# Square roots without ScalarE's table and a causal mask on the exponentials, in a four-layer kernel with a baked order

## The chip, the cores and the metric

The kernel runs on one core of one Trainium2 chip, in one launch. The metric is the device time in microseconds (us). The engines are TensorE (PE, with its weight loads PEld), VectorE (DVE), ScalarE (ACT), GpSimd (POOL) and SyncE (SP, which issues most transfers).

## The reference, cut to what matters

The input is two sequences of 1024 tokens with 128 features, in fp32. Four layers follow each other; each takes the layer norm of x and adds a product of two branches:

```python
for layer in range(4):
    xn = layernorm(x)                  # 1 / sqrt(var + 1e-5)
    s  = attention_branch[layer](xn)
    g  = silu(feedforward_branch[layer](xn))
    x  = x + s * g
```

- Layer 0: a delta-rule attention in chunks of 32 tokens with q and k of unit length, `beta = sigmoid(xn @ Wb)`, short convolutions, a router that mixes four outputs, and RMS norms; its other branch has silu and gelu.
- Layer 1: softmax attention with 16 heads of 8 features, with scores divided by a Frobenius norm (a root), and a mixture of eight experts, two per token.
- Layer 2: linear attention with 16 heads of 64, and a small transformer on 63 chosen tokens with RMS norms.
- Layer 3: causal attention with 16 heads of 64 that share k and v, q and k of unit length, and two blocks of windowed attention with rotary positions, norms of q and k, a layer norm and a gated gelu.

The causal attention of layer 3 is where the mask of this change lies:

```python
q, k = l2norm(q) * 4, l2norm(k) * 4
sim  = einsum('bhid,bjd->bhij', q, k)
sim  = where(j > i, -max, sim)
out  = einsum('bhij,bjd->bhid', softmax(sim), v)
```

## The kernel before, in words

**Recording and order.** The program does not issue instructions as it is written. Each call is recorded as a unit (`Record.note`, line 507; up to 32 matmuls of one kind make one unit), with the tiles that it reads and writes. The units are then issued in an order that is baked into the source as a compressed string (`ORDER`), which a search outside the kernel has found; it also says, for each evacuation that either engine can do (`Ctx.evac`, line 710), whether DVE or ACT does it. A second string (`PLACES`) says which buffer each tile takes. `Record.issue` (line 571) reads both, so nearly every instruction of the profile has line 591. Batch 0 and batch 1, and the two branches of a layer, are interleaved by this order; on each engine the instructions run in it. Each engine class in `Engines` (line 616) has a fixed and a per-element cost for that search, and `TABLES` names the activation functions that need a table of ACT: exp, gelu, silu and sin, sqrt, sigmoid.

**Roots.** `Ctx.rstd` (line 759) and `Ctx.rnorm` (line 766) form one over a root: DVE adds or clamps, ACT takes `Sqrt`, DVE takes the reciprocal. They are used by `layernorm` (line 773; eight columns, 12 times), in layer 0 (the norm of q and k with 64 columns, line 843, and `rms` with 32), in layer 2's `rmsnorm` (one column), in layer 3's causal attention (`rnorm` of k with 4 columns, of q with 64 columns in `Block.scale`), and in layer 3's feed-forward branch (q and k norms with 64 columns in `ss`, and `root` with 4 columns before `roots`). Layer 1 has two single roots on one row (`den`, `q2`). ACT holds one table at a time, so a root between exponentials or gelus needs an `ACT_TABLE_LOAD` before and after it.

**The causal attention.** `l3_attn` (line 1832) goes block of queries by block (`Block(i)`, 512 queries, i = 0, 1) and in each through eight pairs of heads (`pair(p)`). For each tile m of 128 keys up to the diagonal, `scores(m)` makes two score tiles `sim` in PSUM (one for each head of the pair, on half of the array's rows), adds the mask `hide` (0 or -1e30) on DVE to the first 128 columns if the tile is on the diagonal, and lets ACT write the exponential to `e` in SBUF. `sums(m)` multiplies `e` into `num` (a half of the array's columns for each head) and adds `e` to the running total on DVE. Scores of tile m + 1 come ahead of the sums of tile m:

```python
if m >= 4 * i:
    nc.vector.tensor_tensor(ps[a][:, :P], ps[a][:, :P], C.c["hide"], ALU.add)
nc.scalar.activation(es[a][:, :n], ps[a][:, :n], AF.Exp, scale=16.0)
```

There are 2 batches x 2 blocks x 8 pairs x 4 diagonal tiles x 2 heads = 256 such additions. Beside them layer 3's feed-forward branch has its rotation on POOL (`sq`, `u`, 128 and 64 products).

**Layer 0's recurrence.** Each chunk's state follows from the last: four small matmuls `next` on PE, then an addition `state` on DVE, 30 times in each batch. `chunk`, `pu` and `out` are the small matmuls around it.

Of the kernel before, what the change touches and what calls it, by code (L numbers as in the profile page):

```python
# [25 lines left out]
P = 128  # L26
NB = 2
# [172 lines left out]
def _constants():  # L200
# [20 lines left out]
        "hide": np.where(p <= c, 0, -1e30) + 0 * one,  # L221
# [13 lines left out]
        "token": p + P * c[:, :8],  # L235
        "slot": np.where(c < 127, c, -1) + 0 * p,
# [32 lines left out]
def pack_inputs(inputs):  # L269
# [31 lines left out]
TABLES = {AF.Exp: 1, AF.Gelu: 2, AF.Gelu_apprx_tanh: 2, AF.Silu: 3, AF.Sin: 3, AF.Sqrt: 4, AF.Sigmoid: 5}  # L301
# [6 lines left out]
    "c-n1R2V4`$+uqsT6hiNysDQ}XMNm<&on7pLT~G9n1$#wLgaqt@4J)2{cF%%X5DRv|Q&Fs_AfgnJqI3c&yYtP=CJ^rTkz{vgcFNo4dEObdFY(O(YmCLR-|6"  # L308
    "r6zU_|EzXRPL!>Sq4<a1pL{bL+Xk2B|LIdk)T=F$ZFlBZ+nqWJ0cj|yks?PYSWFd((ai60%Kai>R0RngN->g=oOzZ~;Jpk;xxvgkq1-0KS%ZS!xnR`u@Sv"
    "(fR%HKxkWxu?UwmL)`RZ$R5D*hR^(mLoQM(W5qUp7;B_cZNB?Wij-xU5-0mbcNZ#uJo^MjPz~$kD=QR%sVI!0wK)yQY%(kJOAi`xzfeaK(c(LqsZ<haEP4"  # L310
    "~veoH(OI3;Uq&AzM`NUR^cgL!Xz77ojp2)ce`sc~#d#Cze?zVkkcHY`n3&3C=CRp~l7t-yhU($`iFz5_q>Yw)-dMjn%%Hoo>s+d1}zpNN?#%0!$y*axV#<"
    "a?F)6nDZ)ecV{RcRyvDvha1vvA}fvF7*JwWf8_*u$?5iI>Js1GVNx8kMn%XEkmz@QHJI<(b#YsQ$ZCAxAsu<oN0e@_3h0JMA~%48V_O#r4iKB=wnX0my8N"
    "uQ{z-K63rku0;W8@@HO^>kPiRJnLz!1hQ1mNB!>&`s{8}D;5tvXP(~@<lUY-93~y|_8hSZh8CUxb1nJkC6oT4V^*=-=2_KSZ(6e*7=s0hHOFWF4d%yg{d1"
    "neDCtY^(vcG`-929scpj)XfUq#hr*;`P*3@SW{F&Vgl-8MK3Ufy&BHU)4T)Tbh8S#oqm$_LRmvk1tGO;fKZtJ(N+zLQhozr))d!>{1*PabU$dC4$>n?CW1"
    "d42VO)azJueoJWV~@}7_dO@M-~A6RTc%L5+0K!6^w0z#9^x6LHq8ur)F0d{l&Lw<_T5G5(q_#H>SCCe_t>d1`CVc{a>UEu+y*6HQ!W>ptcVRx9dH1od+E&"
    "5{v!Z^Ck*T~_A0*K8)V;WF#yA)18&_M-Dk!eW2YTMhu)N38z@#;C40sBncrBlua~)W#Patmc6+{c8_sXLGQd{T`dzPnww0P*Per@9)f&H>M}iL(SuPaqQE"
    "jX?J2hLXmAV<j*@36FjJhnwlYDlczcc;9-q**bShB48hs0=~v2sb-g}JQrSJ$^)3b*fhqw>x_7%3W+07iO6KJk6g9i;RD$$i1UKB)I6z_h88eHxo-R{hbm"
    "#WxpJmC-Rvtfbq$?b0f-;|FmYfMOt{V@AhM?b3PxWNl#kQ?I2}IWQJi01y!O#zXQP^ca5YxmBCtciwmM3ztV4FP7|`r#uZno9r`>4?7eCD_MyaShF=eUu?"
    "s&KNm%Gs02Z^7XbSsBu)hwAm#u&`dw#ml>rVf^Lns=jqnF+w*j)MOwyJnfluvTbf*F6{|ErJgcfN<T8T&tYMK?MEsa^dV@Yc7n3ZW}EwVtTbmnt`Cu7kr%"
    "~b96Cf<An0O1>m#Pegfe-?pyCg|`nI+Ff#`~Co1Nu3x->KK;yeY%w1qg}P<LkF*P^TVsgy~v#I@@>zuJ)qt(EJXaoHwawGTz5I>7#Mp?SsHYI($6Hnn^Vp"  # L320
    "YzB-=oKgR^@ns0okmu<;2(6h!~Yx%|Xbr*}rof1wTZ+0rM*y5j4*Vumm7-1wnKPI)`#Q>haI{wO}O5_TW)-D0`NCRNx4PaJd)!~`hFNqegD&Y0T`?Z$gMI"
    "Ntcn)ZB!?Bo8??F++zSt;2f;9yy0#Z{Th>Yj_RT4{@)2NaYPIx>NWC3MGkmUW+-S=D#=1l>z3L8XORhY$6#2mO^Iz_rZvyG6Hj{|wAOJ{u2AYE>4o16rsG"
    "I@L=Us5DXW%ug!`y?ah<NQ%$<x~TIXz`n!&7oyP&i}!~_5eqKfFH$c*@4p|g^I~nl=wk~G0iKy3yFg28jJaWV811kdQkvDE5|An(XT^zrnb(=qT(yx{$wA"
    "9XV5v0bL|V=mGFr$>adc@~LzPjUBPZgdxppH`IG$(39L>=6x$Wqj`rov+Z=AI@bfp<x&Oi|l(Hp??#*D1W0wA8K)rdLSl~Ds$_@zXEq(uKDpPQ3-(YcZ4b"
    "gj&|Oy=^D;U^{lY5Nz@sMeCpbufY&EtBtLRS9_7a)I2A(f%|xbNZoSZL`f-8&JYPmba+pt>$klm6~VR0=tY(D}g9V!>kRlHmVS@GKd7Vsxn801rNO7nf6{"
    "UJwz`+#tarRkTX%4BDGimSjcJ^<TXaayy~H0qE<35dh**gtEAQSV&fevv<y_e?-D;Y$F2L)Ud}}i2l5UTD%w^1oIVg)+>L#-HX%c@JScbR=>8gzJl)HVe-"
    "u!5#H#Y%px=gO7w!tCC+0bAo;h_>zui9;?N9CfWRv*cD@%7X@k=+D&)7fLKF`#C(BbwzF3C4<``Pq(<CyCk<^OK><e^Mpz|I3-=xIf*in96M&CQLKcQaQd"
    "h-fWi9kywGVN$14+RROpPPM+V*=)k&6H`4PShJm)b{1)~`6&C@=X2j8#}`VIx{s%K03|g2Wwqkyw~ZSenJ-3Bt5inUGvSV6X_&{X6L9>Azzt#X0cH!_Jv^"
    "oybK)1vS?gtrvs38sO>orH5)(Km!EWklm2BR@O6i;<#&t7JYApj#O+PRvj#o~PQwLmNWPpK2KV?_Z5@VF{{*|`>__zG#T3BK1%$x6fee`9ISw}P5W^<yBA"
    "60ceuYH@v*H10Ge|>&iL@*B>zc0STjK8t}=Ebx7-pFbztfU!M)4n_1Dw{U+4mfFFTbnlA?>c*X*vAzK35VmQe*CdnN1gehx9G{`cPIY5X*BBEphrC1u~f>"  # L330
    "?lomuUlfL$3_&4pP8^SqJ_&Q^)UBp6B=mwEW^tkuZgR<J?F+W;Y{yHt^Rofz}X$F{=Gr){dN=?f(_H?D%NNHchJ{%#dF*R2HjaI%DQq4Xa@n@wI&GC|4r<"
    ")^ann5v716e(!jrn?`kFE^-;+osJT+E_nq5){JRGNac_N%vLF1ouW%Dh_)=qh{C%eX$Zy9K;3rTWIyUltcEd#8@zZug>}47=^~udmrH;A5ExdRVx8Oz!_E"
    "DA)cB7}V`)3m`5wOZO^~f_l@Mv~DuC%(^DWjny2QYqyEzoW@x|$ViKtp`fM29ILJ~fv(>;$qq34tCNi5%`+Wo^N-CXM!=|EV*zQSB9nSsy2QRrOTX*P%hI"
    "}`u-5|1Y6h(lr4i&IFLNy69d8fIb|`!}M#ChCHB*%7T}2$r7umBSj;2or?p|7SCor?^iY>)^Hb%)4eRlTpOH1tFoH!DGEAC}mkl5|z+;3%eSADFCdS3NNZ"
    "`L#4zO{U2dGtzCW6Mvb_ndOY6T7or_bxcx!pGn8!l9U@TYI=%Sl6dMA#)9A1}u*~2wk*)(J(9DG0!Z23z{|{oQ`N6M(^z(|J%$?=g!5Rv3wl+zY~}JKffC"
    "dxIFM%*40J8!sM6D6W^GEkc(X|PJGt$Li<iH7w(+)ZOPnD?SgyfEc^cS>#wcF4}VXdcx5Wj_+K`zlO34?LU%vwbnJhB^?5wTrS9O1bLsb|Hs907;mVBclz"
    "?LQ8hcRKy!vzNs-LZuo5NJ+PbNwV?EFpy-W~kd)brI3Q9(+d=+keagO+t#-D*T_r;RN=UwH=3YEfkDac#^I7mIq;z_^Yzv@-Tos?DZ<-gmjD$jbw-^A{fL"
    "FG}v^Q2by@QvL{s%Tvp$-+Djq-0G~%^X}NI*0n0X=Y7=oz>u2zlkR<U>HMkAv+`}<w^b5V-(=Ou8*_>tmn|-M+EMiOm#l8al}Yh+eUqmi=|1q+#!>I5*Ea"
    "`y=&JdzvwzsN1z*NnmjSEYGvDxE++DLZy|*uuNx<zM|BmSM=coAfA3BWdb~SCoprvEN{I;#AdOpx-%bI)Yf%ki)?L6_}#rF`qWZ$ApQR|%6Ic*T8Z<=wpl"
    "gIK?@7rlhEKO6Nd!+{-g7p0Av(JMM1+U!r0Zhm_=zZhHGv6mKfmgc!<+^`nAK%#Zb@qfyZpK}FpJlXX)(jq;wJanXbpF({vR7=TUl&W!-Nco7t!{UIHS@8"  # L340
    "t(l^8FD6RT8Dsk5Lq6$m=>5z99w*BU}e&0urH-Y_>KKGgBTQZk=Zjt`c9(=G~v8(dL(rr72p4nQvc*UuoV0j8yGQ;Oz(CcY08<)LH_Wm8``rI~QiR*H}nC"
    "^(3pAB};cKvEr?Xk-!OS8QCfsu84qg}y97bbzUH<mOUrj{g6%ddFf(=}gJm*I7CbxP-g=t%QtH4H!S{+JIfe<_Vy<)?a><orEsMCC)#t-T-Xyf3wU;$d|B"
    "kS6`wq;d=6y5^Oc?my3m|J|;xHTdDNZMZ}8{UfScmi+5%^i}2i(pBly<pA(D`uaFLu{>z|NcNlTGpIIeVfhZ>bGs`;bANi;yaTHqTizL4nBV2v+HFgsCBI"
# [12 lines left out]
    "Q{4*c+A>;jO=+#awl*9JAn<p@B+T7?hA~)G)=vzzr@^8&~rq3Ij<kYzz#NNG5cD-imoyzx4^G;@cjgnt2e!_M-x?IJ}_&r|zMKEb}VsDKE$l^zoTiqGMGj"
    "+5`{jS22Rz#GSSr53{y!Ul5bleqMd&7Uk|BeNNp?N(!t=j^Er7>{Llvf`-KlB(G!TUN~2|9Kv&t<cTpJ;WTF<)MF@mMtH-LePor&jTn=Enleb8O-V-l=De"
    "KDIC(lsMe-%;=j##Tv$}a*ta8E$(+OJ$HPwq8IM=7P(fB3dcB9h%Qw?38OVZ+fjDm_p26_gSyLC@w@Ev*YUf>H2wg(|D!o}ML8G#Y@XQl?cfmq9`fb3b+2"
    "3Jb^^wKMwWf;`gj0>gQNjk5l9`F>3+wh+!}t>j{NMVdhPoJ)YK15DVgy|tWoxT_c^foa!22vrb&)&vPV74m5lUpPez(rW$FH<YjR(e$~>*JjJ`Tn!=y5$W"
# [266 lines left out]
class Ctx:  # L626
# [132 lines left out]
    def rstd(self, out, ss, scale, eps):  # L759

        nc = self.nc
        nc.vector.tensor_scalar(out, ss, float(scale), float(eps), ALU.mult, ALU.add)
        nc.scalar.activation(out, out, AF.Sqrt)
        nc.vector.reciprocal(out, out)
# [1555 lines left out]
```

## Time and profile before

| | |
|---|---|
| median of 3 runs | 1816.81 us (1807.41 to 1821.72) |
| profiled execution | 1815.64 us, span 1813.9 us |
| mean granted TensorE clock | 0.967 |
| busy PE / PEld | 1700.4 / 956.8 us |
| busy DVE / ACT / POOL | 1270.4 / 1045.7 / 417.9 us |
| `ACT_TABLE_LOAD` | 101, 1283 ns each |
| mask additions `sim<-sim,const` on DVE | 256, 293 ns each |
| sums `e<-e` on DVE (128 to 512 columns) | 320, 167.0 us in all |

In a line of the profile the line number and the engine come first, then the operation, the tile that is written and those that are read, the shapes, the count, and after the bars the busy time with the mean of one in ns, and the engine's idle time before these instructions with what ended it. In the rows of 40 slices a digit is the busy share in tenths. An fp32 matmul shows as two passes and a transpose as one, so 7750 instructions are 14500 records. Passes of matmuls overlap in the records.

### The profile page before, as it was taken

The page shows a single profiled execution, that of the slowest core. Times are in us where ns is not written, and L with a number is a line of the kernel's source. Part 1 is how long each engine was busy: PE and PEld are TensorE (multiplying, and loading weights), DVE is VectorE, ACT ScalarE, POOL GpSimd, SP SyncE. Part 2 cuts the span into 40 slices and gives each one's busy share as a digit, 9 for nine tenths or more (in the row PEclk, how much of TensorE's full clock was granted, in tenths as well). Part 3 has the DMA queues.
Part 4 walks back from the last instruction along what each step waited for, and adds up shares of the span by engine and source line. Part 5 has one row for each costly group of instructions (what it writes and reads, how often), then busy time and mean ns, then how long its engine had stood idle before and what let it go on. Part 6 is the DMA issues. An engine that isn't in the chain of part 4 may idle for free. (4 is left out here: it accounts for less than half of the span.)

```text
span 1813.9 us, 36041 instructions
## 1 busy us (share of the span) xinstructions
PE 1700.4 (94%) x14500; PEld 956.8 (53%) x14500; DVE 1270.4 (70%) x2546; ACT 1045.7 (58%) x1907; POOL 417.9 (23%) x450
## 2 busy tenths in 40 slices
PE   7997998798999999999988989999999899999998
PEld 4464445565234943358455457753436567643376
DVE  7855587476212634425889989978798989887875
ACT  4221452246888579865646546576555668775653
POOL 1110013002502245112211253040601740540000
PEclk9996999788999999999999989999999999999999
DMA  2110002000503224224131123202004231001131
GB/s 109 21 31 3 0 7 42 15 1 20 170 12 115 71 81 104 69 84 146 28 109 33 46 60 100 69 12 61 4 1 112 69 83 52 4 4 46 24 95 37
DMA packets 82407, 97.55 MB, mean 54 GB/s; under 512 B 39584, under 2 KB 51872, under 8 KB 82112
## 3 DMA queue, kind: packets, MB, share of 16 engines
q1 hardware_dynamic: 73120, 65.92, 13.1%
q0 software_dynamic: 9120, 29.33, 5.8%
q8 instruction: 114, 1.87, 0.4%
q14 instruction: 53, 0.43, 0.1%
HBM read 79.84 MB, written 6.98 MB: 48 GB/s over the span
## 5 line engine op out<-in xcount | busy, mean ns | idle before, releaser
L591 ACT ACTIVATE e<-sim 128x512 f32<-128x512 f32 (+3 forms) x896 | 428.5, 561 | 151.9 <-PE sim L591 59.6
L591 DVE TENSOR_TENSOR e<-e 128x512 f32<-128x512 f32 (+3 forms) x320 | 167.0, 547 | 13.9 <-ACT e L591 6.2
L591 PE MATMUL num<-e,v 128*64 128x64 f32 (+4 forms) x1280 | 168.7, 386 | 0.4 <-ACT e L591 0.2
L591 ACT ACT_TABLE_LOAD x101 | 129.6, 1283 | 53.3 <-PE sim L591 8.8
L591 PE MATMUL sim<-q,k 32*128 32x512 f32 x1024 | 156.2, 636 | 2.9 <-DVE place L591 1.2
L591 PE MATMUL sim<-q,kT 64*128 64x512 f32 (+3 forms) x768 | 149.4, 511 | 3.1 <-ACT e L591 1.8
L591 POOL TENSOR_TENSOR sq<-qk,tab 128x256 f32<-128x256 f32 x128 | 102.5, 824 | 166.3 <-DVE ss L591 135.1
L591 PE MATMUL av<-e,va 128*32 128x512 f32 x1024 | 130.7, 602 | 0.0
L591 PEld LDWEIGHTS num<-e,v 128*64 128x64 f32 x1280 | 75.6, 137 | 85.7 <-issue 66.5
L591 PE MATMUL ph<-h,w_f 128*128 128x512 f32 x256 | 117.7, 616 | 3.1 <-ACT h L591 2.3
L591 PEld LDWEIGHTS sim<-q,kT 64*128 64x128 f32 x768 | 66.8, 186 | 82.9 <-ACT e L591 49.3
L591 PEld LDWEIGHTS sim<-q,k 32*128 32x128 f32 x1024 | 48.8, 183 | 93.8 <-ACT e L591 73.3
L591 POOL TENSOR_TENSOR u<-u,sq 128x512 f32<-128x512 f32 x64 | 85.4, 1349 | 1.6
L591 DVE TENSOR_TENSOR sim<-sim,const 128x128 f32<-128x128 f32 x256 | 65.7, 293 | 27.4 <-PE sim L591 25.4
L591 DVE SCALAR_TENSOR_TENSOR conv<-vT,w_a,conv 128x1024 f32<-128x1024 f32 x60 | 82.9, 1389 | 1.3
L591 PEld LDWEIGHTS ph<-h,w_f 128*128 128x128 f32 x256 | 49.3, 197 | 63.2 <-issue 57.8
L591 POOL DMA_INDIRECT xg<-xd,token x46 | 45.3, 985 | 139.8 <-ACT e L591 102.8
L591 ACT ACTIVATE e<-e 128x512 f32<-128x512 f32 x96 | 57.0, 625 | 26.2 <-DVE e L591 25.6
L591 DVE COPY asb<-av 128x512 f32<-128x512 f32 x16 | 11.0, 685 | 84.1 <-PE av L591 75.5
L591 PEld LDWEIGHTS av<-e,va 128*32 128x32 f32 x1024 | 23.6, 108 | 81.2 <-issue 68.1
L591 ACT ACTIVATE h<-ph,w_f 128x512 f32<-128x512 f32 x32 | 21.2, 687 | 78.2 <-PE ph L591 78.2
L591 PE MATMUL qk<-w_f,shifted 128*128 128x512 f32 x128 | 62.9, 608 | 2.7 <-DVE shifted L591 1.4
(543 smaller groups left out, 3523.2 us busy)
## 6 DMA issues: line engine op xcount, KB each, us to landing
zb<-zd SPq DMA_DIRECT2D x192, 128.0 KB
w<-v SPq DMA_DIRECT2D x60, 128.0 KB
tab<-in_rotary SPq DMA_DIRECT2D x8, 512.0 KB
yd<-y SPq DMA_DIRECT2D x10, 256.0 KB
w_f<-in_f SPq DMA_DIRECT2D x4, 512.0 KB
w_l<-in_l SPq DMA_DIRECT2D x4, 512.0 KB
mk<-in_mask SPq DMA_DIRECT2D x4, 512.0 KB
w_f<-in_f SPq DMA_DIRECT2D x4, 448.0 KB
```

The source lines that it names most:

```text
L591: tc.keep_in_program_order(f(*map(real, args), **{k: real(v) for k, v in kw.items()}))
```

## The change

1. `rstd` becomes two instructions on POOL: add epsilon, then raise to the power -1/2 against a new constant `mhalf`. The scale 1/n goes into the `Square` activation ahead of it. `rnorm` does the same for up to eight columns (k's norm); for 64 columns it clamps on DVE and calls `rsqrt`.
2. `rsqrt` is new: a first value from the bits of the number (a multiply-add on them as an integer), then three Newton steps of three DVE instructions each. It serves q's norms in layer 3, and the norm and `rms` of layer 0.
3. Layer 1's two roots become powers with `phalf` on POOL; one of them, and the mean square of layer 3's `root`, is copied from PSUM by DVE first.
4. Layer 0's sigmoid is written as (1 + tanh(x/2))/2. `Sqrt` and `Sigmoid` leave `TABLES`.
5. The mask of the causal attention moves behind the exponential: POOL's `affine_select` writes 0 where the key is later than the query. The constant `hide` goes.
6. `ORDER` and `PLACES` are new strings for the new set of units; all units stand in a new order, and 16 more evacuations are on ACT in place of DVE. `Record.issue` passes on a bit cast.

```diff
-TABLES = {AF.Exp: 1, AF.Gelu: 2, AF.Gelu_apprx_tanh: 2, AF.Silu: 3, AF.Sin: 3, AF.Sqrt: 4, AF.Sigmoid: 5}
+TABLES = {AF.Exp: 1, AF.Gelu: 2, AF.Gelu_apprx_tanh: 2, AF.Silu: 3, AF.Sin: 3}
...
-    def rstd(self, out, ss, scale, eps):
+    def rstd(self, out, ss, eps):
+
+        nc, n = self.nc, ss.shape[-1]
+        nc.gpsimd.tensor_scalar(out, ss, float(eps), None, ALU.add)
+        nc.gpsimd.tensor_tensor(out, out, self.c["mhalf"][:, :n], ALU.pow)
+
+    def rnorm(self, out, ss, floor):
+
+        nc, n = self.nc, ss.shape[-1]
+        if n <= 8:
+            nc.gpsimd.tensor_scalar(out, ss, float(floor), None, ALU.max)
+            nc.gpsimd.tensor_tensor(out, out, self.c["mhalf"][:, :n], ALU.pow)
+            return
+        x = self.small("x", n)
+        nc.vector.tensor_scalar_max(x, ss, float(floor))
+        self.rsqrt(out, x)
+
+    def rsqrt(self, out, x):
 
         nc = self.nc
-        nc.vector.tensor_scalar(out, ss, float(scale), float(eps), ALU.mult, ALU.add)
-        nc.scalar.activation(out, out, AF.Sqrt)
-        nc.vector.reciprocal(out, out)
-
-    def rnorm(self, out, ss, floor):
-
-        nc = self.nc
-        nc.vector.tensor_scalar_max(out, ss, float(floor))
-        nc.scalar.activation(out, out, AF.Sqrt)
-        nc.vector.reciprocal(out, out)
+        t = self.small("t", x.shape[-1])
+        nc.vector.tensor_scalar(out.bitcast(I32), x.bitcast(I32), -0.5, 1597463007.0, ALU.mult, ALU.add)
+        for _ in range(3):
+            nc.vector.scalar_tensor_tensor(t, out, -0.5, out, ALU.mult, ALU.mult)
+            nc.vector.tensor_mul(t, t, x)
+            nc.vector.scalar_tensor_tensor(out, t, 1.5, out, ALU.add, ALU.mult)
...
-    nc.scalar.activation(beta, psb[:, :NTH], AF.Sigmoid)
-    nc.vector.tensor_mul(beta, beta, rk)
-    nc.vector.tensor_mul(beta, beta, rk)
+    nc.scalar.activation(beta, psb[:, :NTH], AF.Tanh, scale=0.5)
+    nc.vector.scalar_tensor_tensor(beta, beta, 1.0, rk, ALU.add, ALU.mult)
+    nc.vector.scalar_tensor_tensor(beta, beta, 0.5, rk, ALU.mult, ALU.mult)
...
-    nc.scalar.activation(q2, q2, AF.Sqrt)
+    nc.gpsimd.tensor_tensor(q2, q2, C.c["phalf"][:1], ALU.pow)
...
                 for a in range(2):
+                    nc.scalar.activation(es[a][:, :n], ps[a][:, :n], AF.Exp, scale=16.0)
                     if m >= 4 * i:
-                        nc.vector.tensor_tensor(ps[a][:, :P], ps[a][:, :P], C.c["hide"], ALU.add)
-                    nc.scalar.activation(es[a][:, :n], ps[a][:, :n], AF.Exp, scale=16.0)
+                        nc.gpsimd.affine_select(
+                            out=es[a][:, :P], in_=es[a][:, :P], compare_op=ALU.is_ge, fill=0.0, base=0,
+                            pattern=[[1, P]], channel_multiplier=-1,
+                        )
...
-            C.rstd(r, pn[:, :4], 1.0, 1e-5)
+            nc.vector.tensor_copy(r, pn[:, :4])
+            C.rstd(r, r, 1e-5)
```

## The prediction

> **What bounds the kernel now.** I read the page's first two parts, then the windows by layer, then the PE timeline inside two stages, and last the chain and the groups. From the page:
>
> ```profile
> PE 1700.4 (94%) x14500; PEld 956.8 (53%) x14500; DVE 1270.4 (70%) x2546; ACT 1045.7 (58%) x1907; POOL 417.9 (23%) x450
> ...
> PE   7997998798999999999988989999999899999998
> ...
> DVE  7855587476212634425889989978798989887875
> ACT  4221452246888579865646546576555668775653
> POOL 1110013002502245112211253040601740540000
> PEclk9996999788999999999999989999999999999999
> ```
>
> PE is nearly always busy, but busy is not streaming. In the PE timeline 15 passes of ph (128x512) end 6.60 us after the first starts, and one lasts 0.62, so a full pass costs (6.60 - 0.62)/14 = 0.43 us; 16 passes of 128x128 take 1.95 us, so 0.11 each. Counting all 14,500 passes of the groups by form at this rate, a tile of a quarter of the array at a quarter, gives 1447 us. So 1814 - 1447 = 367 us are lost, only 114 of them shown as idle. The windows say where (layer 0, 1, 2, 3, then the two spans that hold the 256 masks of layer 3's causal attention):
>
> ```profile
> 0.00:450.00 450.00, 394.49 (x4632) 235.50 (x4632) 304.93 (x603) 155.36 (x244) 54.72 (x71) 0.90 0.11 25
> 450.00:850.00 400.00, 396.48 (x3084) 194.70 (x3084) 152.60 (x369) 303.37 (x565) 114.66 (x123) 1.00 0.32 92
> 850.00:1150.00 300.00, 273.07 (x1745) 167.23 (x1743) 264.87 (x475) 173.44 (x288) 80.93 (x79) 0.97 0.24 67
> 1150.00:1814.00 664.00, 636.33 (x5043) 359.36 (x5043) 547.97 (x1100) 413.54 (x814) 167.56 (x177) 0.99 0.16 44
> ...
> 1190.00:1370.00 180.00, 176.55 (x969) 77.16 (x969) 153.45 (x352) 113.51 (x246) 48.20 (x49) 0.99 0.07 20
> 1585.00:1765.00 180.00, 178.90 (x1432) 86.87 (x1430) 147.15 (x341) 113.26 (x245) 25.34 (x30) 1.00 0.14 39
> ```
>
> Columns after the length: busy PE, PEld, DVE, ACT, POOL, then the granted clock. Layer 0 streams about 296 of 450 us: latency (a recurrence of small matmuls) and a clock of 0.90. Layer 1 streams 332 of 400, beside exponentials that keep ACT at 76%. Layer 2 streams 244 of 300, with DVE at 88%. Layer 3 streams 575 of 664, and PE leads there with DVE at 83% close behind. A part of the loss is in the order itself:
>
> ```profile
> 507.50 1.06 PE L591 MATMUL av<-e,va 128*32 128x512 f32 x8
> 508.50 1.14 PE L591 MATMUL sim<-q,k 32*128 32x512 f32 x8
> 509.57 1.92 PE L591 MATMUL av<-e,va 128*32 128x512 f32 x16
> 511.42 1.14 PE L591 MATMUL sim<-q,k 32*128 32x512 f32 x8
> ```
>
> Eight passes on four parts of the array should take 2 x 0.43 = 0.86 us. From start to start av takes 1.00, sim 1.07, but sixteen av in a row 1.85, not 2.00. Each change of tile shape costs about 0.15 us.
>
> **The change, part by part.** The counts are from the two kernels' instruction lists.
>
> *Tables.* ACT's loads go from 101 to 43, and 48 small root and sigmoid activations go or become a tanh.
>
> ```profile
> L591 ACT ACT_TABLE_LOAD x101 | 129.6, 1283 | 53.3 <-PE sim L591 8.8 <-DVE bq L591 7.4 <-DVE lg L591 7.0
> ...
> L591 DVE TENSOR_TENSOR sim<-sim,const 128x128 f32<-128x128 f32 x256 | 65.7, 293 | 27.4 <-PE sim L591 25.4 <-ACT e L591 1.0
> ...
> L591 POOL TENSOR_SCALAR gains<-w_a,gain 128x128 f32<-128x128 f32 x1 | 0.6, 610 | 8.9 <-DMA w_a<-in_a 8.9
> ```
>
> 58 x 1.283 = 74 us leave ACT. The Trainium skill ("ScalarE: Activation LUTs", What ACT_TABLE_LOAD costs) prices a switch at 2.66 us, load and drain; that would be 154 us. The trace has no such drain: a copy ends at 45.16 us, a load starts at 45.17 and the next activation at 46.47, 1.30 us in all. I take the row. ACT also loses some 10 us of roots and gains 16 evacuations from DVE (16 x 0.59 = 9). But ACT bounds only stretches of layer 1 that have hardly a load. What counts is what lay on the path. The chain of waits reaches back over the last 357 us; 20 loads start there, and it holds three as pieces of their own (3.8 us), such as:
>
> ```profile
> 1475.76 1.28 ACT L591
> 1477.05 0.70 ACT u L591
> ```
>
> Three in 20, each 1.3 us: 58 x 0.15 x 1.3 = **-11 us**. A gelu's load can remain where exponentials came before, so I take **-8**; the ends are 0 and -20.
>
> *Masks.* 256 additions on DVE go (256 x 0.293 = 75 us), and 256 selections come on POOL, after the exponential. No row shows a selection. Below: COPY 128x64 on POOL takes 0.24 alone (0.38 mean). Nearest: TENSOR_SCALAR 128x128, 0.55 and 0.61. Above: the skill ("GPSIMD Engine Reference", 3.1) gives about 12 cycles an element at 1.2 GHz to data-dependent branching, so by estimate 128 x 12/1.2 = 1.3 us, with 0.3 to start 1.6. I take 0.55: 141 us on POOL. In the instruction list 234 of the 256 stand right behind another selection and only 22 behind other work. From the score matmul to the first product with its exponential the new PE order holds at least 2.9 us of streaming for these tiles, against exponential 0.6 + selection 0.55 + two hand-overs of some 0.1; so the added step is hidden by the pairs ahead of it. If that cover went, it would cost up to 0.5 us a pair, 128 pairs, 64 us.
>
> The same page (1, SBUF interfaces) speaks against the move: POOL contends with DVE instructions that have two SBUF inputs. The trace agrees:
>
> ```profile
> 1604.77 1.28 POOL L591 TENSOR_TENSOR u<-u,sq 128x512 f32<-128x512 f32 x1
> ...
> 1605.40 1.06 DVE L591 TENSOR_TENSOR e<-e 128x384 f32<-128x384 f32 x1
> ```
>
> That sum takes 0.55 with POOL quiet. All 320 such sums (e<-e) stand in the mask spans, where POOL is busy 74 of 360 us now (20%) and 215 (60%) after. 320 x 0.4 more encounters x half a selection (0.28) = 36 us back on DVE. By the rule left out, the masks would free 75 us of DVE; with it, 39.
>
> *Roots.* 16 Newton chains (14 on 128x64, 2 on 128x32) have 11 small DVE operations each, at 0.19 (state 128x32, 0.190) 2.1 us, for a floor (0.19 alone, 0.50 mean) and a reciprocal (0.54): net +1.2 x 16 = 20 us of DVE. The 28 small ones move to POOL as add and power: DVE -11. With 16 evacuations moved off it (-11), DVE changes by -75 + 36 + 20 - 11 - 11 = -41 us, from 83% to about 76% in the mask spans. A power has no row either; TENSOR_TENSOR 128x1 on POOL takes 0.19, and I take 0.4 for 128x8 (bounds 0.2 and 1.5). Add and power with two hand-overs then last as long as floor, root and reciprocal did (0.17 + 0.21 + 0.20 and hand-overs): 0, ends -5 and +30 (28 x 1.1). What queues behind a waiting power is POOL's rope (1.35 us) or gathers (0.95), seldom what PE needs next. DVE is 2% of the chain, PE 16% of its 20%; a tenth of the 41 us: **-4 us**.
>
> *Order.* PE has the same 7750 matmuls but 485 changes of tile shape for 595: 110 x 0.15 = **-16 us**, 75 of them in layer 3; the ends are 0, if PE waited there anyhow, and -19. Of each batch's recurrence of 120 next matmuls in layer 0, the stretch from first to last held 2.9 and 6.0 us of streaming and now holds 9.7 and 12.9. PE waits 14.5 us for DVE's state there: up to -14, I take half, **-7**. SP's queue carries the same 500 transfers; the constants shrink by 104 columns.
>
> Sum: -8 - 4 - 16 - 7 = -35. The profiled execution took 1815.6 (span 1813.9), 1.2 under the median, so **1780 us**, 2% less.
>
> **The rivals.**
>
> 1. *Covered* (0.22). Where the loads and masks lay under PE, and where shape changes fell into waits, only the recurrence and part of the loads count: -3 to -12, about 1808. For: PE is 98% busy in the mask spans. Against: it streams only 318 of those 360 us.
>
> 2. *POOL's price* (0.14), slower. The selections sit in two spans of 180 us, 128 each, beside 25 to 48 us of rope: (180 - 37)/128 = 1.1 us. From there POOL, not PE, ends these spans. At 1.6 us: 128 x 1.6 + 37 = 242, so 62 us a span, 124 in all, less half of it that the interleaved feed-forward takes up, less the 35: about 1842. For: nothing measured lies above 0.61 at this size. Against: exactly that row, and the rule is for branches.
>
> 3. *Relief compounds* (0.14). Layers 2 and 3 lose 56 + 89 = 145 us. If a third of that (48) goes with the lighter DVE and ACT, where the sum above takes about 4 + 5 + 11 from it, it is 28 us more: about 1752, and with 10 more in layer 0 1742. For: DVE is the second engine in both layers. Against: 2% of the chain is DVE's.
>
> **How the numbers follow.** Main forecast 0.50 (1760 to 1797), rivals 0.22, 0.14, 0.14. A measurement of this kernel tells about 1% from nothing (18 us). Faster: main and rival 3, 0.64; same: rival 1, 0.22; slower: 0.14. The range 1742 to 1825 leaves out rival 2 and the far end of rival 3.
>
> **What would show it.** Right: table loads near 55 us; DVE busy near 1230; POOL near 570 with selections of 0.5 to 0.6 us; x16 runs of sim and num in the mask spans; 1150 to the end shorter by some 20 us; layer 0 by some 8. Wrong: selections over 1 us, or e<-e sums whose mean rises by more than 0.2 us with idle time of PE before num behind POOL; powers of several us before a layer's first transposes; or PE's wait for DVE unchanged at a lower DVE load, which is rival 1.

## The result, and the profile after

The changed kernel takes **1823.31 us** (median of 20 runs, 1813.59 to 1831.58) beside 1816.88 for the kernel before: a ratio of **1.0042, 95% interval 1.0025 to 1.0059**. A second time it was 1.0029 (1.0014 to 1.0045); below I take 1.0035 for it. The forecast was 1780: 2% less came out as 0.4% more. The profiled execution took 1813.6 us. It is the fastest of its 20, some 10 under their median, so its times are set against each other here, not against the medians.

The page after, its first two parts:

```profile
PE 1679.1 (93%) x14500; PEld 955.0 (53%) x14500; DVE 1270.2 (70%) x2374; ACT 970.9 (54%) x1817; POOL 587.3 (32%) x766
...
PE   6998989879999999999999889999899899899997
...
DVE  6865697486123555146999998769968999867765
ACT  3232322228887588844646455655446466555642
POOL 1020112034023352215002651546534632862301
PEclk9998889889999999999999899999999999999999
```

ACT lost 75 us, as reckoned. POOL gained 169 where about 150 was expected, and not as expected: the selections took 32 us less than reckoned, the powers far more. DVE is as busy as before (1270.2 for 1270.4), although 172 instructions fewer run on it, the mask additions (65.7 us busy) among those that left. About 1230 was expected. The same by layer, in the windows (columns as before):

```profile
0.00:450.00 450.00, 396.74 (x4729) 237.31 (x4729) 319.26 (x666) 149.59 (x252) 80.67 (x96) 0.93 0.14 35
450.00:850.00 400.00, 395.73 (x3072) 198.46 (x3069) 158.41 (x358) 298.95 (x559) 126.70 (x128) 1.00 0.29 86
850.00:1150.00 300.00, 275.36 (x1939) 178.80 (x1938) 276.30 (x494) 161.93 (x274) 86.08 (x86) 0.97 0.22 65
1150.00:1814.00 664.00, 611.26 (x4766) 340.44 (x4764) 516.22 (x858) 360.40 (x735) 293.84 (x459) 0.98 0.15 41
```

The first three windows hold more passes of matmuls than before (9740 for 9461): the kernel is ahead when it comes to layer 3. I counted the streaming of each kernel's matmuls at the rates of the prediction (0.43 us for a full pass) and asked when each had streamed as much. After 1000 of the 1447 us, early in layer 3, the changed kernel is 30.0 us ahead, after 1200 it is 19.6 ahead, at the end 2.1. **The gain was made, and layer 3 gave it back.**

The 28 us lost in layer 3 are firm, the 30 before it are not. A second execution of the same kernel (after_again, 1821.7 us) is 22.5 ahead after 1000 us and 5.9 behind at the end, so it loses the same 28. Its lead is smaller because layer 0 went slower: after 320 us of streaming, three executions with the same layer 0 (after, after_again, a_newton0) are 14, 10 and 1 us ahead of the kernel before, at granted clocks of 0.93, 0.91 and 0.89 in the first 450 us, where the kernel before had 0.90. So some 20 us are nearer to the lead that the change itself made. In layer 3 the windows have the clock at 0.98 for 0.99; by estimate, 1% of the 575 us that stream there, this makes up to 6 of the 28 us, and no run separates it.

The groups that carried the prediction:

```profile
L584 DVE TENSOR_TENSOR e<-e 128x512 f32<-128x512 f32 (+3 forms) x320 | 174.0, 581 | 59.2 <-PE num L584 33.1
...
L584 POOL TENSOR_SCALAR_AFFINE_SELECT e<-e 128x128 f32<-128x128 f32 x256 | 108.6, 451 | 170.5 <-ACT e L584 152.9
...
L584 ACT ACT_TABLE_LOAD x43 | 55.2, 1283 | 32.3 <-DVE h L584 11.7
```

Loads (55.2 us), selections (0.451 us, 0.55 reckoned) and sums (174.0 us, only 7 more than before) cost no more than reckoned. What does stands lower down. POOL's powers, in the groups by form:

```profile
L584 POOL TENSOR_TENSOR ln_r<-ln_r,const 128x8 f32<-128x8 f32 x12 | 20.5, 1711 | 0.8
...
L584 POOL TENSOR_TENSOR par<-par,const 1x16 f32<-1x16 f32 x4 | 11.8, 2952 | 66.3 <-DVE row L584 64.3 <-DVE par L584 2.0
...
L584 POOL TENSOR_TENSOR root<-root,const 128x4 f32<-128x4 f32 x8 | 9.9, 1241 | 0.7
...
L584 POOL TENSOR_TENSOR r<-r,const 128x4 f32<-128x4 f32 x4 | 4.1, 1034 | 0.3
...
L584 POOL TENSOR_TENSOR r<-r,const 128x1 f32<-128x1 f32 x4 | 2.3, 584 | 0.2
```

These are 32 powers. One takes 1.7 us at 128x8, where 0.4 was taken; all of them take 49 us (20.5 + 11.8 + 9.9 + 4.1 + 2.3; the other groups here are no powers). And the Newton chains of layer 3, on DVE:

```profile
L584 DVE TENSOR_TENSOR t<-t,x 128x64 f32<-128x64 f32 x36 | 17.8, 494 | 0.9
L584 DVE SCALAR_TENSOR_TENSOR t<-r 128x64 f32<-128x64 f32 x36 | 14.0, 389 | 0.8
L584 DVE SCALAR_TENSOR_TENSOR r<-t,r 128x64 f32<-128x64 f32 x36 | 12.7, 352 | 0.9
L584 DVE TENSOR_SCALAR x<-ss 128x64 f32<-128x64 f32 x12 | 8.9, 743 | 0.3
...
L584 DVE TENSOR_SCALAR r<-x 128x64 int32<-128x64 int32 x12 | 5.6, 464 | 0.3
```

These 132 instructions take 59 us; at their median of some 0.22 it would be 29. What stretches them is in the timeline. A line gives the start, the length, and the instruction:

```profile
1276.57 0.61 DVE L584 TENSOR_SCALAR r<-x 128x64 int32<-128x64 int32 x1
1277.21 1.26 POOL L584 TENSOR_TENSOR u<-u,sq 128x512 f32<-128x512 f32 x1
1277.22 1.34 DVE L584 SCALAR_TENSOR_TENSOR t<-r 128x64 f32<-128x64 f32 x1
...
1278.59 0.22 DVE L584 TENSOR_TENSOR t<-t,x 128x64 f32<-128x64 f32 x1
...
1278.69 1.26 POOL L584 TENSOR_TENSOR u<-u,sq 128x512 f32<-128x512 f32 x1
1278.85 1.18 DVE L584 SCALAR_TENSOR_TENSOR r<-t,r 128x64 f32<-128x64 f32 x1
...
1281.69 1.22 DVE L584 TENSOR_TENSOR u<-u,r 128x1024 f32<-128x1024 f32 x1
...
1283.09 1.23 DVE L584 TENSOR_TENSOR u<-u,r 128x1024 f32<-128x1024 f32 x1
1284.23 2.49 DVE L584 TENSOR_TENSOR e<-e 128x512 f32<-128x512 f32 x4
1285.01 0.98 ACT L584 ACTIVATE e<-sim 128x512 f32<-128x512 f32 x2 [6.41 <-DVE e L584]
...
1285.66 3.36 PE L584 MATMUL sim<-q,kT 64*128 64x512 f32 x8 [6.30 <-ACT e L584]
```

A step that starts while POOL's product u runs (1277.22, 1278.85) ends just after POOL does, 1.3 and 1.2 us instead of 0.22. This holds for all 16 of the 108 steps on 128x64 that start beside a u: they end 0.08 to 0.16 us after it. The 62 steps with POOL idle take 0.22 on the mean, 27 that overlap a u 0.80, eight beside the product sq 0.57; five beside a power take 0.22.

Behind the chain, on the same queue, stands the sum e<-e. ACT has waited 6.41 us for it with its next exponential, and PE 6.30 us for ACT. Of ACT's wait the chain takes 3.1 us (from 1278.59 to 1281.69), and about 2.5 go to two products u<-u,r that need roots and stood on DVE before the change too. This is one place; layer 3 loses 28 us. But it shows a way of the loss: a chain of tiny steps, some stretched by POOL, ahead of what the attention needs.

### The profile page after: what moved, and what is told of

Same layout as the page of the kernel before. It is cut to its first block, busy times and chain, and to the rows that moved or that the text cites. A ratio compares the mean times of both kernels' runs of the same rounds, so it can differ in the third digit from the quotient of the medians.

```text
span 1811.9 us, 36210 instructions
## 1 busy us (share of the span) xinstructions
PE 1679.1 (93%) x14500; PEld 955.0 (53%) x14500; DVE 1270.2 (70%) x2374; ACT 970.9 (54%) x1817; POOL 587.3 (32%) x766
## 5 line engine op out<-in xcount | busy, mean ns | idle before, releaser
L584 DVE TENSOR_TENSOR e<-e 128x512 f32<-128x512 f32 (+3 forms) x320 | 174.0, 581 | 59.2 <-PE num L584 33.1
L584 POOL TENSOR_SCALAR_AFFINE_SELECT e<-e 128x128 f32<-128x128 f32 x256 | 108.6, 451 | 170.5 <-ACT e L584 152.9
L584 PE MATMUL sim<-q,k 32*128 32x512 f32 x1024 | 145.9, 641 | 1.9 <-DVE place L584 1.3
L584 PEld LDWEIGHTS num<-e,v 128*64 128x64 f32 x1280 | 80.4, 139 | 90.2 <-issue 52.1
L584 PEld LDWEIGHTS sim<-q,k 32*128 32x128 f32 x1024 | 42.5, 185 | 90.9 <-ACT e L584 74.9
L584 POOL DMA_INDIRECT we<-in_experts,expert x46 | 45.1, 980 | 128.5 <-PE qk L584 58.7
L584 ACT ACT_TABLE_LOAD x43 | 55.2, 1283 | 32.3 <-DVE h L584 11.7
```

Source lines behind the costliest of these rows:

```text
L584: tc.keep_in_program_order(f(*map(real, args), **{k: real(v) for k, v in kw.items()}))
```

## The experiments

In all of them the order of units stays as it is in the kernel named. A unit's instruction is emptied (`nothing()`) or another put into its place (`add`). Tiles and the work of all other units stay; only b_all, b_roots and a_best have two small buffers more, which all their added chains share. Except where said, the edits are to the changed kernel. Four kernels (marked *) ran on a chip where the kernel before took 1889 us and the changed kernel wasn't beside it, so only their ratios are used, and with care: two of them, run again where the kernel before takes 1816 to 1818 us (the usual time below), went from 0.994 to 0.999 (a_newton2) and from 0.990 to 0.993 (a_pow).

| run | what differs | table loads | ratio to before (95%) | median us |
|---|---|---|---|---|
| after_again | nothing | 43 | 1.0029 (1.0014 to 1.0045) | 1822.3 |
| a_mask | mask by DVE before exp | 43 | 1.0634 (1.0597 to 1.0672) | 1934.4 |
| a_newton0 | 12 chains of layer 3 without steps | 43 | 0.9877 (0.9845 to 0.9910) | 1797.1 |
| a_both | both of these | 43 | 1.0475 (1.0432 to 1.0517) | 1902.0 |
| b_all | old order; roots and mask changed | 47 | 1.0327 (1.0295 to 1.0359) | 1877.9 |
| a_actroot * | those 12 by ACT's table | 61 | 0.9941 (0.9913 to 0.9968) | 1880.9 |
| a_newton2 * | two steps in all 16 | 43 | 0.9938 (0.9915 to 0.9960) | 1878.3 |
| a_newton0_ffn * | 8 of the 12 without steps | 43 | 0.9869 (0.9835 to 0.9902) | 1867.9 |
| a_pow * | powers become products | 43 | 0.9901 (0.9874 to 0.9929) | 1871.6 |
| a_n0pow | a_newton0 and a_pow | 43 | 0.9807 (0.9781 to 0.9834) | 1782.2 |
| a_best | two steps; small roots by chains on DVE | 43 | 1.0202 (1.0169 to 1.0234) | 1854.9 |
| b_mask | old order; only the mask changed | 101 | 1.0047 (1.0020 to 1.0074) | 1825.2 |
| a_actall | all roots by ACT's table | 96 | 1.0150 (1.0112 to 1.0189) | 1844.9 |
| a_n2act | two steps; small roots by ACT's table | 85 | 1.0148 (1.0117 to 1.0179) | 1843.3 |
| a_newton2_b | two steps in all 16 | 43 | 0.9989 (0.9971 to 1.0007) | 1815.2 |
| b_roots | old order; only the roots changed | 47 | 1.0373 (1.0343 to 1.0404) | 1883.7 |
| a_newton1 | one step in all 16, tuned constants | 43 | **0.9946** (0.9930 to 0.9962) | 1808.0 |
| a_pow_b | powers become products | 43 | 0.9929 (0.9901 to 0.9956) | 1804.5 |

**Mask or chains?** Theory S made the selection the culprit, theory N the Newton steps.

a_mask puts the addition of `hide` back ahead of the exponential, in the exponential's place:

```diff
                     nc.scalar.activation(es[a][:, :n], ps[a][:, :n], AF.Exp, scale=16.0)
                     if m >= 4 * i:
+                        u = C.record.units[-1]
+                        head = ps[a][:, :P]
+                        u.ops.insert(0, ("vector:tensor_tensor", (head, head, C.c["hide"], ALU.add), {}))
...
+                        C.record.nothing()
```

> The changed kernel in its own order, with one part undone: the mask is again an addition on DVE ahead of the exponential, in the place of the exponential's unit, and the 256 selections on POOL are gone. Theory S (the selection on POOL, as one more link between exponential and product, loses what layers 0 to 2 gained): about 20 us less than the changed kernel, near 1803 us, and the lead at equal streaming stays near 30 us in layer 3. Theory N (the Newton chains, whose small DVE instructions wait for POOL's rope one by one, lose it): no gain, rather 5 to 15 us more, since DVE has 75 us more to do.

S fell, and by far: 1.063, 6% more where it foretold 1% less. N had the direction, but not the size. PE's waits, the longest of this kernel (the columns: us in total, times, longest), and the same wait in the changed kernel:

```profile
PE sim L601 <- ACT e L601: 72.4, 39, 6.9
...
PE sim L584 <- ACT e L584: 13.3, 12, 6.3
...
PE num L584 <- POOL e L584: 4.4, 6, 1.6
```

In the kernel before this wait adds up to 2.1. In the new order a mask on DVE ahead of the exponential queues behind whatever stands on DVE, and the exponential with it; the selection comes after the exponential. This run adds a link that the order was not made for, so by itself it does not clear the selection. What speaks for its innocence is the last line, from the changed kernel: PE waits 4.4 us in all for a selected e.

a_newton0 empties the nine steps of the 12 chains on q's norms in layer 3 (4 in the causal attention, 8 in the feed-forward), so that their first rough value is the root:

```diff
-        self.rsqrt(out, x)
+        self.rsqrt(out, x, False)
...
             nc.vector.scalar_tensor_tensor(t, out, -0.5, out, ALU.mult, ALU.mult)
+            if not steps:
+                self.record.nothing()
```

> The changed kernel in its own order, where the 12 chains of 128x64 in layer 3 keep the first value from the bits and leave the three Newton steps out (108 DVE instructions fewer; the norms of q and k are then only good to a few per cent). Theory N: 12 to 20 us less than the changed kernel, near 1808 us, with the wait of 6.3 us of PE near 1280 us gone. Theory S: at most 5 us less.

N held: 0.9877, more than the 12 to 20 us it foretold. The wait of 6.3 us near 1280 us is gone:

```profile
PE sim L600 <- ACT e L600: 7.7, 13, 1.6
```

The 108 instructions, 44.5 us of busy DVE (17.8 + 14.0 + 12.7) and 20.5 at the 0.19 of the prediction, were worth 1.0035 - 0.9877 = 1.6%, 29 us by the medians. The profiled execution (1804.6 us, the slowest of its six) gives less: layer 3 loses 14 us from 1000 us of streaming on, where the changed kernel loses 28. So 14 to 29 us, many times the 2 that the prediction had for all 16 chains.

a_both has both edits:

> Both of these: the mask on DVE ahead of the exponential and no Newton steps in layer 3 (those roots only good to a few per cent). If S and N each hold a part, about 30 us less than the changed kernel, near 1793 us; if one alone holds, no better than that one alone.

At 1.0475 neither forecast came. It is 1.6% under a_mask, so the steps cost the same with either mask; and it is 6.0% over a_newton0, so what the mask on DVE costs in this order does not come from the steps.

**Order.** b_all is the kernel before, in its own order, with roots, sigmoid and mask of the changed kernel, each in the place of what it replaces:

```diff
         nc.scalar.activation(out, out, AF.Sqrt)
+        self.record.nothing()
+        add("gpsimd:tensor_tensor", out, out, self.c["mhalf"][:, :n], ALU.pow)
...
+                        C.record.add(
+                            "gpsimd:affine_select", out=es[a][:, :P], in_=es[a][:, :P], compare_op=ALU.is_ge, fill=0.0,
...
```

> The kernel before in its own order and with its buffers, with all roots and the sigmoid changed (POOL powers, Newton chains in one piece) and the mask as a selection on POOL right behind the exponential. If the 30 us gained in layers 0 to 2 are the new order's, this one is 20 to 40 us slower than before, near 1845 us; if they are the table loads', it is near the changed kernel, 1815 to 1825 us.

1.0327, 62 us more than before where 20 to 40 were foretold. So the new units cost 3.3% where they were not planned for, and the new order brings 1.0327 - 1.0035 = 2.9% of it back. The chains are not placed as in the changed kernel: here each stands in one piece, on buffers that all chains share. What part of the 3.3% this makes was not tried.

b_mask takes the mask alone into the old order:

> The kernel before in its own order and with its roots by ACT, with the mask alone moved: no addition on DVE, a selection on POOL right behind the exponential. If the selection (0.45 us in the trace after, and one more hand-over) is hidden by the pairs ahead of it: 0.99 to 1.00 of before, for DVE's 75 us. If the link is late in an order that was not made for it: 1.01 to 1.02.

It is 1.0047, no gain, and between its two forecasts. Its page shows what was freed:

```profile
PE 1703.7 (94%) x14500; PEld 959.1 (53%) x14500; DVE 1226.0 (67%) x2290; ACT 1044.2 (57%) x1907; POOL 522.4 (29%) x706
```

DVE has 44 us less to do than before, and the time is not shorter. Whether these 44 us bounded nothing in the old order, or the longer way through POOL took back what they gave, is not separated.

b_roots takes the roots and the sigmoid alone into the old order:

> The kernel before, its order and its mask, with all roots changed as in the changed kernel: Newton chains of three steps in layer 3, powers on GpSimd. Theory R (roots cost by themselves, in either order, some 40 us of chains and powers, less the 54 table loads that go): 1.010 to 1.030. Rival: the roots are hurt only by the new order's crowding of GpSimd: 0.995 to 1.003. The old order with roots and mask changed was 1.033, the mask alone 1.005.

1.0373, more than either forecast: the roots, with 54 table loads gone, cost 3.7% there. With the new mask beside them (b_all) it is 0.5% less, hardly more than the two intervals allow. PE waits 9.8 us at one place for DVE's q, a wait that the kernel before doesn't have:

```profile
PE g L610 <- DVE q L610: 9.8, 1, 9.8
```

By equal streaming this kernel is 24.8 us behind after 320 of 1447 us (layer 0's chains and norms), 41 after 1000, and 71 at the end.

**Other ways to a root, in the new order.** The first four ran on the other chip.

a_actroot: a_newton0, with `Sqrt` on ACT and the reciprocal on DVE in the place of the first value.

> The changed kernel in its own order, with the 12 chains of 128x64 in layer 3 undone: clamp on DVE, square root by ACT's table, reciprocal on DVE, so 61 table loads in place of 43. If the Newton chains cost because they hold DVE: about 20 us less than the changed kernel, near 1802 us, the 18 loads and 12 reciprocals giving back some 5 of the 26 us that leaving the steps out gave. If the roots themselves were what mattered (any root late by several us), no gain, near 1820 us.

a_newton2: the third step of all 16 chains emptied (`if k == 2: self.record.nothing()`).

> The changed kernel with two Newton steps in place of three in all 16 chains (48 DVE instructions fewer, roots good to a few millionths). If the price goes with the number of instructions: about a third of the 26 us, so 8 to 10 us less, near 1814 us. If only the first ones matter, that wait for POOL's running instruction: under 3 us.

a_newton0_ffn: a_newton0 for the eight chains of the feed-forward alone.

> The changed kernel with the steps left out in the eight chains of the feed-forward branch alone, whose rope runs on POOL; the four of the causal attention keep them (the norms of the eight only good to a few per cent). If contention with the rope is the price: nearly all of the 26 us, near 1799 us. If the number of instructions is: two thirds, near 1806 us.

a_pow: `ALU.pow` becomes `ALU.mult` everywhere, so no roots are taken there; place, engine and shape stay. (The DVE instruction of 7.5 us that the forecast names stood beside products and fills, not behind a power: see the last section.)

> The changed kernel with each power on POOL turned into a product of the same shape (all roots of up to 16 columns are then wrong). The trace has the powers at 0.6 to 3.0 us, 49 us in all, and DVE instructions of up to 7.5 us behind them. If they matter: 8 to 15 us less than the changed kernel, near 1811 us; if they are hidden, within 3 us of it.

Table (0.9941) and two steps (0.9938) are equal. Ratios stand 0.3% (a_pow) to 0.5% (a_newton2) lower on this chip. So a_newton0_ffn's 0.9869 is 0.990 to 0.992 at the usual time: eight of the twelve chains bring 73 to 87% of what all twelve bring. That lies between two thirds (the count of instructions) and nearly all (the rotation, or rope, on POOL), and does not decide between them.

after_again is the control at the usual time.

> The changed kernel itself, once more beside the kernel before on the chip of these runs, as the base for the others here: ratio 1.004, if the chip with the lower clock of the last runs (before at 1889 us) shifts both alike; below 1.000 there if a lower clock favours the changed one, which has less on ACT and DVE.

a_n0pow takes both suspects away at once; it leaves out the steps of the 12 chains and the powers:

> The changed kernel with both costs taken away: no Newton steps in layer 3 (norms of q and k only good to a few per cent) and each power on POOL a product (the small roots wrong). If the two add up: 0.965 to 0.975 of before, which is where the prediction stood (0.980); if they hide each other, no better than 0.985.

**0.9807, 1782.2 us**: with the two terms gone the kernel stands at the forecast, though not at the 0.965 to 0.975 that stood for a full sum of both. By equal streaming it is 41.0 us ahead after 1000 us and 33.9 at the end, so layer 3 keeps most of the lead. It still gives back 7 us where the prediction had it gain 20, and the layers before it gain far more than the 15 that were left for them.

a_best was to be the better kernel: two steps, and the small roots as chains of eight DVE instructions (nine in layer 1), with no power on POOL.

```diff
+        add("vector:tensor_copy", x, out)
+        add("vector:tensor_scalar", out.bitcast(I32), x.bitcast(I32), -0.5, 1597463007.0, ALU.mult, ALU.add)
+        for _ in range(2):
+            add("vector:scalar_tensor_tensor", t, out, -0.5, out, ALU.mult, ALU.mult)
+            add("vector:tensor_mul", t, t, x)
+            add("vector:scalar_tensor_tensor", out, t, 1.5, out, ALU.add, ALU.mult)
```

> A complete version: the changed kernel with two Newton steps in place of three, and no power on POOL; the small roots are Newton chains of two steps on DVE in the place of the power. DVE gets some 32 chains of 8 instructions at 0.16 us (41 us), POOL loses 49 us of powers. If it is POOL's hold on DVE that costs: 0.980 to 0.990 of before, better than both kernels. If DVE's own time is what counts: 0.995 or more.

I was wrong: 1.0202. The powers are slow, but the chains are worse. Before the products `roots` of layer 3 alone PE now waits 18.0 us, in seven places, for the small root, 2.9 in the changed kernel:

```profile
PE roots L600 <- DVE root L600: 18.0, 7, 5.7
```

a_actall goes the other way: the table for every root, in the new order.

```diff
         nc.gpsimd.tensor_tensor(out, out, self.c["mhalf"][:, :n], ALU.pow)
+        self.record.nothing()
+        self.record.add("scalar:activation", out, out, AF.Sqrt)
+        self.record.add("vector:reciprocal", out, out)
```

> The changed kernel, its order of units and its selection on GpSimd, but with every root of layer 3 and every power back where the kernel before had them: a square root by ScalarE's table and a reciprocal on VectorE, in the place that the Newton steps or the power have in the new order (about 90 table loads again). Theory R (the new way of taking roots is the loss; order and selection are a gain that it eats): 0.980 to 0.995 to before, about 1795. Rival O (the order is made for roots without table loads and gains nothing with them): 1.000 to 1.015.

a_n2act does that to the small roots only, with two steps in the long chains:

> The changed kernel with two Newton steps in place of three in the sixteen long chains, and the small roots (all 28 powers) by ScalarE's table and a reciprocal. Complete to the accuracy of the kernel before. From a_newton2 (0.994) and a_pow (0.990 without the powers' price at all): 0.985 to 0.995 if the small roots' table loads (about 1.3 us each, two a root, most beside other work) cost less than the powers do; over 1.000 if they cost as much.

1.0150 and 1.0148. Theory R ("the new roots are the loss") is too simple: a_actall came out where its rival O had it, at the upper end, and a_n2act on the side where the loads cost as much as the powers or more. In a_actall too PE waits before `roots`:

```profile
PE roots L600 <- DVE root L600: 11.5, 6, 3.7
```

Against a_newton2_b, a_n2act has 42 loads more and no power for 32 (the forecast says 28), and is 1.6% (29 us) slower. With two steps in the long chains, small roots by power, table and chain stand at 0.9989, 1.0148 and 1.0202: in this order a power is the cheapest of the three.

a_newton2_b repeats a_newton2 at the usual time:

> The kernel of a_newton2 (two Newton steps in the sixteen long chains) beside a run of before at its usual time: the ratio measured on the slower chip, 0.994, stands if the ratio does not depend on the chip; 1.000 or more if a_newton2's gain was the other chip's.

0.9989: the same as before, and 0.5% under the changed kernel. The 0.994 of the other chip did not carry over.

a_pow_b repeats a_pow there:

> The kernel of a_pow at the chip's usual time: the changed kernel with every power on GpSimd computed as a product, so with wrong roots, everything else as it is. The prediction valued the powers at nothing: then it stays at 1.003. If the powers cost what a_n0pow leaves beside a_newton0 (0.981 against 0.988), 0.996; if their delays and those of the chains need each other, above 1.000.

0.9929, lower than all three forecasts: the powers' price alone is 1.1%, 19 us, although POOL is busy for only a third of the span. It is not paid by holding DVE: none of the 66 DVE instructions that start while a power runs in the changed kernel takes over 1.5 times the shortest of its kind (the median is 1.01 times). What is left is what waits for the root, and what stands behind the power on POOL's queue; how much each makes was not tried.

a_newton1 keeps one step in each of the 16 chains, with constants tuned for one (relative error of a root up to 0.00065):

```diff
-        nc.vector.tensor_scalar(out.bitcast(I32), x.bitcast(I32), -0.5, 1597463007.0, ALU.mult, ALU.add)
+        nc.vector.tensor_scalar(out.bitcast(I32), x.bitcast(I32), -0.5, 1595932665.0, ALU.mult, ALU.add)
...
-            nc.vector.scalar_tensor_tensor(t, out, -0.5, out, ALU.mult, ALU.mult)
+            nc.vector.scalar_tensor_tensor(t, out, -0.703952253, out, ALU.mult, ALU.mult)
...
-            nc.vector.scalar_tensor_tensor(out, t, 1.5, out, ALU.add, ALU.mult)
+            nc.vector.scalar_tensor_tensor(out, t, 1.68191391, out, ALU.add, ALU.mult)
```

> The changed kernel with one Newton step in each of the sixteen long chains, with the three constants of the chain tuned for one step (relative error of a root up to 0.00065), so 6 dependent VectorE operations fewer in a chain than in the changed kernel. None of the steps gave 0.988 and three gave 1.003 to 1.004, two gave 0.999: if each step costs its share, one step gives 0.993 (0.990 to 0.996) and is faster than both kernels; if the place and number of what waits there matter more than the count of operations, 0.998 or more.

**0.9946**: faster than both kernels, by 0.5% and 0.9%, with no part of the computation left out. Three, two and one step give 1.0035, 0.9989 and 0.9946: each step of 48 instructions costs 0.44%, 8 us, which is 0.17 us an instruction. So a step is paid at about its length beside an idle POOL (0.19 to 0.22), less than half of what it takes on the mean in layer 3 (0.41). By this price the 108 steps of a_newton0 would be 18 us, within the 14 to 29 above. Its page and its steps:

```profile
PE 1680.2 (93%) x14500; PEld 960.9 (53%) x14500; DVE 1247.5 (69%) x2278; ACT 971.1 (54%) x1817; POOL 592.5 (33%) x766
```

```profile
L600 DVE TENSOR_TENSOR t<-t,x 128x64 f32<-128x64 f32 x12 | 6.3, 526 | 0.4
...
L600 DVE SCALAR_TENSOR_TENSOR t<-r 128x64 f32<-128x64 f32 x12 | 5.3, 439 | 0.2
...
L600 DVE SCALAR_TENSOR_TENSOR r<-t,r 128x64 f32<-128x64 f32 x12 | 4.5, 376 | 0.3
```

The count fell from 36 to 12 of each kind, and the mean stayed (0.53, 0.44 and 0.38 us for 0.49, 0.39 and 0.35): what POOL does to a step hardly depends on how many there are.

## Why the prediction was wrong, step by step

- **Roots: this step failed, with two terms of its sum.** (1) The chains were put down as +20 us of DVE, of which "a tenth" was to reach the end, 2 us. Three steps in all 16 cost 24 us (three times 8, a_newton1), those of the 12 long ones alone 14 to 29 (a_newton0). Their length was off (44.5 us busy for the steps at 20.5 reckoned), but most of it is the share: a third to two thirds of the 44.5 reached the end. The tenth came from the chain that ended last in the kernel before. The lines are of before, after, and after_again:

```profile
PE 16%; DVE 2%; ACT 1%; issue 0%; POOL 0%; DMA 0%; DVEq 0%; ACTq 0%; POOLq 0%
...
PE 21%; DVE 18%; POOL 3%; issue 3%; ACT 2%; DMA 1%; SPq 1%; POOLq 0%; DVEq 0%; ACTq 0%
...
PE 1%; DVE 1%; issue 0%; POOLq 0%; POOL 0%; ACT 0%
```

  These are shares of the span, and the chain reaches back a different way each time: 357 us, 912 us and, for the same changed kernel, 44 us. DVE holds 2 of 20% before, 18 of 50% after. A share that hangs on where the chain breaks off is no price for new work on that engine.

  (2) The powers were taken at 0.4 us, within bounds up to 1.5, and valued at 0. They take 0.58 to 2.95 us, beyond the upper bound at 128x8 and 1x16, and cost 19 us alone (a_pow_b), 13 where the steps are gone too (a_newton0 against a_n0pow). The bound of +30 held them; the choice within it did not, since the row that it was taken from was a product. How one reaches the path shows in the layer norm, here in the view by tile:

```profile
L584 POOL TENSOR_TENSOR ln_r<-ln_r,const x12: 1666/1674/2119, 10.6 to 1794.4; 128x8 f32<-128x8 f32 x12
```

  Add and power take 1.92 us by their medians (0.244 + 1.674), where addition, root and reciprocal took 0.58 (0.172 + 0.208 + 0.203). DVE sits idle 6.8 us for it in all, before four of the twelve products that need it.
- **The two together** are 1.0035 - 0.9807 = 2.3%, 41 us: the whole distance from 1823 to 1782. So the other terms are right in sum to a few us, but not by stage. Of the 35 us foretold, 20 were to come in layer 3 and 15 before it; without steps and powers layer 3 loses 7 and the rest gains 41 (a_n0pow, one execution). That the sum fits is in good part luck, and what layer 3 lacks of its 20 us stays open.
- **Tables.** The count was right; -8 for 58 loads was not measured by itself. a_n2act pays 29 us for 42 loads with their roots, beside powers; how much of it comes from an order that does not plan for loads is not shown.
- **Masks.** The selection's length (0.451, reckoned 0.55) and its cover were right: PE waits only 4.4 us for it in all. The 36 us that POOL was to put back on the sums were too many, 7 came. But the same contention, which the prediction counted for the sums alone, fell on the small instructions instead, 30 us of it on the chains. So DVE was not relieved at all, where -41 was reckoned; the -4 drawn from that was small, and its loss with it.
- **Order and recurrence.** PE's wait for the state fell from 14.5 to 9.4 us, 5 of the 7 reckoned. The 20 us that layer 3 was to gain turned into a loss of 28. About half of that loss goes with the steps (a_newton0 loses 14) and a quarter with the powers (a_n0pow loses 7).
- **Small slips in the working.** The additions of the mask are 65.7 us of busy time, since their records overlap; 75 is the sum of their lengths. There are 32 powers, not 28, with the four of layer 1. Of the 320 sums 308 lie in the two mask spans. None of them moves the forecast by more than a few us.
- **The rivals.** None of the three was it. Rival 2 saw POOL's price, but in the selections, where nothing was wrong. The chance of 0.14 for slower was put there. Of the signs of being wrong, "powers of several us before a layer's first transposes" came nearest: the layer norm's takes 1.7 us. The mechanism that was missing: work moved *onto* an in-order queue as many short dependent steps, right ahead of sums that PE's next exponentials wait for.

What stays open: the worth of the new order by itself, since each order here fits its own set of units, and four exchanges cost 1.5 to 6% (b_all, b_roots, a_mask, a_actall), though b_mask cost 0.5%. How much of the steps' price is their count and how much POOL's stretching was not separated: no run had the steps without the rotation beside them. Slower kernels also have a lower granted clock here (a_mask 0.943, b_roots 0.950, the kernel before 0.967, in their profiled executions), and no run tells how much of their time is that. And whether an order searched for one step and powers, or for a_actall's units, would be faster was not tried.

## What to carry to other kernels

Price a replacement by its count of dependent instructions on the queue where it lands, and by what stands behind it there, not by the share that this engine had in the old critical chain. Here three steps in 16 chains cost 24 us of kernel time. Twelve roots by table, with 18 loads of 1.3 us, did as well as two steps in place of three in all chains (a_actroot and a_newton2). Take no price of an unknown operation from the cheapest row of the same instruction name: a power and a product are both TENSOR_TENSOR, and here a power took three to fourteen times as long as a product of the same shape. Where an approximation is iterated, cut the iterations to what the precision needs before anything else is moved.

## What was not expected of the hardware

- The time of a power on GpSimd goes with the columns, and no effect of the partitions shows: 0.58 us at 128x1, 1.03 and 1.24 at 128x4, 1.71 at 128x8, 2.95 at 1x16, so about 0.16 us for each further column. The same instructions as products take 0.20 at 128x1, 0.20 and 0.41 at 128x4, 0.25 at 128x8 and 0.21 at 1x16 (a_pow_b).
- A product of 128x512 on GpSimd holds up VectorE's small instructions until it ends (the 16 steps above end 0.08 to 0.16 us after it), a power does not (the 66 instructions above).
- VectorE's small instructions can wait out several GpSimd instructions in a row, also with one tensor as input. One of 1x16, 0.99 us in the other batch and 0.16 in the kernel before, takes 7.47 here while three products and two long fills (MEMSET) follow each other on POOL without a gap. It is on the way to PE, whose wait there was 5.3 us before:

```profile
390.35 1.96 POOL L584 TENSOR_TENSOR pr<-mid,lg 128x1024 f32<-128x1024 f32 x1
390.52 7.47 DVE L584 TENSOR_SCALAR par<-par 1x16 f32<-1x16 f32 x1
...
392.27 1.95 POOL L584 TENSOR_TENSOR pr<-o,lg 128x1024 f32<-128x1024 f32 x1
...
394.19 1.95 POOL L584 TENSOR_TENSOR pr<-vtok,lg 128x1024 f32<-128x1024 f32 x1
...
396.13 2.04 POOL L584 MEMSET wide<- 128x1024 f32 x3
...
399.90 0.63 PE L584 MATMUL tr<-par,const 1*128 1x32 f32 x2 [7.73 <-DVE par L584]
```

- It goes both ways: a selection takes 0.29 us with DVE quiet (81 of 256), 0.53 on the mean where DVE runs beside it, and 3.08 at most.
